# Normalized rows through DRAM and transposed on VectorE in the middle groups, with all weights in the order 8p + c

## The chip, the cores and the metric

The kernel runs on one core of a Trainium2 chip. A core has five engines that run their own instruction queues in order and wait on one another by semaphores: TensorE (PE; its weight loads are listed apart as PEld), VectorE (DVE), ScalarE (ACT), GpSimd (POOL) and SyncE (SP), which here issues nearly all DMA transfers. The metric is the time of one launch on the device in microseconds, as the median of several runs.

## The reference

The input has 16 batches of 128 rows by 1024 columns, and a context of the same shape. The computation is one cross-attention block and one FFN block, both with a residual:

```python
x = x + xattn(layernorm(x), ctx, Wq, bq, Wk, bk, Wv, bv, Wo, bo)
x = x + scale * (ei(layernorm(x)) @ kernel)
# xattn: Q = q @ Wq + bq (32 heads of 32), K, V = ctx @ Wk + bk, ctx @ Wv + bv (8 heads of 32)
#        y = softmax(Q K^T / sqrt(32)) V;  result y @ Wo + bo
# ei:    the last 205 of the 1024 input columns are multiplied by -4
```

Everything is float32; the FFN kernel holds only zeros and ones. A matmul contracts over the 128 partitions, so a row that is to be multiplied by a weight has first to be transposed: its 1024 columns go to 8 chunks of 128 partitions. Which column lies on which partition of which chunk is free, as long as the weight's rows are laid out in the same order.

## The kernel before

**Groups.** Two batches form a group; there are eight groups, 0 to 7. While PE does the attention of group g in four quarters (`attend`: scores `sc`, maximum `negm`, exponentials, `inv` and the division `p`, transposes `tpp`, product `av`), the gaps are filled with dense work from a queue: the output projection of group g-1 (`o_u`, `o_v`, `o_c`), keys and values of group g+1 (`k`, `v`), the FFN of both batches of group g-1 (`f`), and the queries of group g+1 (`q_u`, `q_v`, `q_c`). Query and output projections of a group are Winograd-like: seven products of half-size blocks in place of eight, with sums of weight blocks (`combine`) that are made once on DVE and kept in DRAM.

**Order.** All of it is one manual schedule. `Stream` holds a queue of generators, each of which issues a piece of PE work and yields its supposed length in us, and a list of events (`stream.later(us, fn)`), which issue work of other engines when the supposed clock passes them. So the order of each engine's queue is fixed when the program is built; on the chip each engine takes its instructions in that order and waits where data are not there. `length` is the supposed length of a quarter.

**Rows and their transposes.** A row block of x is loaded (`load_x`), normalized on DVE and POOL in place (`norm_x`, two `bn_stats`, then `normalize`), and transposed on PE: eight 128x128 transposes per batch, four into one PSUM tile `tp_x`, which ACT copies to `xT` (`turned`, line 310). The FFN's rows `x2n` are transposed in the same way (`ffn_transpose`, line 646); ACT copies the PSUM tile `tp_f` to `x2h` and DVE subtracts to get the rest `x2l` (line 649), so that the FFN is two fast matmuls. PSUM tiles `tp_x`, `tp_f`, `tpp` and `av` share one pool of two buffers.

The context is transposed otherwise: it is loaded in four DMAs, each of which brings one quarter of the columns for all 128 rows to one quadrant of 32 partitions (`load_ctx`), so that DVE's transposes of 32x32 blocks (line 319) finish the job. Its tile is ordered [partition, 4 row blocks, 8 chunks, 32 columns], so each 32x32 block is contiguous in a partition. The rows of Wv and Wk are brought to the matching order in four DMAs each (`load_by_quadrants`); Wq and the FFN kernel have the order c*128 + p.

**The queue of transfers.** SP issues in order. Weight pieces of 512 KB (`piece`, a ring of eight) are fetched as earlier ones are used up (`fetch`), in the query and output projections. Each SP transfer signals one of eight semaphores in turn and waits for the transfer that used that semaphore before, eight places ahead of it.

In a middle group the dense work is added in this order:

```python
once(get_x, nxt * GB, 14.0),
once(prep_ctx, nxt, 3.7, 8.0, 13.0, 18.0),
os[grp - 1],
once(get_ctx, nxt + 1),
prep_k(nxt),
mixed(prep_v(nxt), chain(ffn_transpose(p0), ffn_transpose(p1)), 1, 2),
once(get_x, nxt * GB + 1, 5.0),
```

and then `ffn(p0)`, `ffn(p1)` with the first half of `prep_x` mixed in, the residual loads, the second half of `prep_x` and the queries `qs[nxt]`. So the first x row is loaded before the output projection and normalized 14 us of supposed time later; the second after the values.

Of the kernel before, what the change touches and what calls it, by code (L numbers as in the profile page):

```python
# [17 lines left out]
P = 128  # L18
# [64 lines left out]
def kernel(  # L83
# [67 lines left out]
    def load_ctx(b, queues=(nc.sync,)):  # L151
        c_t = work.tile([P, NB, NC, 32], FP, tag="ctx", name=f"ctx{b}", bufs=2)
        src = key_value[b].rearrange("(t r) (k c f) -> k r t (c f)", r=32, k=NB, c=NC)
        for k in range(NB):
            dst = c_t[k * 32 : (k + 1) * 32].rearrange("r t c f -> r t (c f)")
            queues[k % len(queues)].dma_start(out=dst, in_=src[k])
        cs[b] = c_t

    def load_by_quadrants(dst, w, queues):
        src = w.rearrange("(k c f) n -> k f c n", k=NB, f=32)  # L160
        for k in range(NB):
            queues[k % len(queues)].dma_start(out=dst[k * 32 : (k + 1) * 32], in_=src[k])

    def load_x(b):

        x_t = work.tile([P, D], FP, tag="xn", name=f"xn{b}", bufs=3)
        nc.sync.dma_start(out=x_t, in_=x[b])
        xns[b] = x_t
# [16 lines left out]
    load_by_quadrants(wv_sb, Wv, two)  # L185
    load_ctx(1, two)
    load_by_quadrants(wk_sb, Wk, two)
# [33 lines left out]
    def q_block(r, o, k):  # L221

        src = Wq.rearrange("(r c p) n -> r p c n", r=2, p=P)[r]
# [20 lines left out]
    def load_ffn():  # L244
        fw = ffn_w.rearrange("(c p) n -> p c n", p=P)
# [5 lines left out]
    def convert_ffn():  # L251

        row_w = const.tile([P, 1], FP, name="row_w")
        nc.gpsimd.memset(row_w, 1.0)
        nc.gpsimd.affine_select(
            out=row_w,
            in_=row_w,
            compare_op=ALU.is_ge,
            fill=w_inh,
            base=n_exc % P - 1,  # L260
            pattern=[[0, 1]],
            channel_multiplier=-1,
        )
        def chunk_(c):
            raw = raws[c // (NC // 2)][:, c % (NC // 2)]
            if (c + 1) * P <= n_exc:
                nc.scalar.copy(wf_sb[:, c], raw)
            else:
                w = w_inh if c * P >= n_exc else row_w
                nc.scalar.activation(wf_sb[:, c], raw, AF.Copy, scale=w)  # L270

        for c in range(NC):
            stream.later(2.0 * c, lambda c=c: chunk_(c))

# [25 lines left out]
    def turned(store, srcs, grp, h, name, batches=range(GB)):  # L300
# [3 lines left out]
        for j in batches:  # L304
# [3 lines left out]
            for c in range(HC):  # L308
                at = (h * HC + c) * P
                nc.tensor.transpose(tp[:, c], src[:, at : at + P], ident)  # L310
# [3 lines left out]
    def turn_ctx(b, h):  # L314
        grp, j = b // GB, b % GB
        if (grp, h) not in cTs:
            cTs[grp, h] = work.tile([P, HC, T], FP, tag="tT", name=f"cT{grp}_{h}", bufs=3)
        src = cs.pop(b) if h == 1 else cs[b]
        nc.vector.transpose(
            cTs[grp, h][:, :, j * S : (j + 1) * S].rearrange("p c (t n) -> p t c n", t=NB),  # L320
            src[:, :, h * HC : (h + 1) * HC],
        )
# [9 lines left out]
    def chunk(store, grp, c):  # L332
        return store[grp, c // HC][:, c % HC]

# [216 lines left out]
    def weighted(b, a, pts):  # L551
# [11 lines left out]
        yTs[b, a] = work.tile(S4, FP, tag="yT", name=f"yT{b}_{a}", bufs=7)  # L563
# [4 lines left out]
    def out_proj(grp):  # L568
# [12 lines left out]
        def run():  # L581
# [36 lines left out]
            def read(mm, c):  # L618
# [7 lines left out]
                if c in ("c12", "c21"):  # L626
                    x2n = work.tile([P, D], FP, tag="xn", name=f"x2n{b0 + j}", bufs=3)
                    x2ns[b0 + j] = x2n
                    us = 3.0 if c == "c12" else 4.5
                    stream.later(us, lambda: normalize(x2n, x_t, stats[j], f"f{b0 + j}"))  # L630
# [4 lines left out]

    def ffn_transpose(b):

        hi = work.tile([P, NC, S], FR, tag="x2h", name=f"x2h{b}", bufs=2)
        lo = work.tile([P, NC, S], FR, tag="x2l", name=f"x2l{b}", bufs=2)
        src = x2ns.pop(b)  # L640
        x2Ts[b] = (lo, hi)
        for h in range(NC // 4):
            tp = ps_tp.tile([P, 4, P], FP, tag="tp", name=f"tp_f{b}_{h}")
            for j in range(4):
                c = 4 * h + j
                nc.tensor.transpose(tp[:, j], src[:, c * P : (c + 1) * P], ident)  # L646
            cut = slice(4 * h, 4 * h + 4)
# [284 lines left out]
```

## Time and profile before

| What | Value |
|---|---|
| time, median of 3 runs | 819.83 us (819.57 to 819.86) |
| the profiled execution: its time, its span | 817.83 us, 816.1 us |
| granted TensorE clock | 1.000 |
| PE busy with matmuls | 789.8 us (97%) |
| PE transposes `tp_x`, line 310 | 128, 18.2 us busy |
| PE transposes `tp_f`, line 646 | 128, 19.3 us busy |
| DVE transposes of the context, line 319 | 32 of 128x512, 698 ns each |
| ACT copies `xT` and `x2h` | 32 each of 128x512, 590 ns each |
| DVE subtraction `x2l`, line 649 | 32 of 128x512, 692 ns each |
| x rows, issue to landing | 16 of 512 KB, median 5.4 us |
| context quadrants, issue to landing | 128 KB, median 5.9 us |
| stores of out, issue to landing | 512 KB, median 2.7 us |

The page lists busy time by engine, the span in 40 slices, the DMA queues, the chain of work that ended last, the costliest groups of instructions, and the transfers. Beside it the trace gives timelines (start, length, engine, line, operation, and in brackets the idle time before it with what ended it), tables of busy time in chosen stretches, and lists of waits. Matmuls are pipelined and the column of their lengths overlaps: what one costs is read from start to start.

### The profile page before, as it was taken

The numbers are of one execution on the slowest core, as the hardware profiler recorded it, in microseconds if no ns is written. First come the engines' busy times: TensorE is split into PE (matmuls) and PEld (weight loads), VectorE is DVE, ScalarE is ACT, GpSimd is POOL, SyncE is SP. The second block draws the span as 40 slices with busy tenths as digits, with TensorE's granted clock in tenths as the row PEclk, the third lists the DMA queues.
The fourth block names the chain that finished last, engine by engine and source line by source line (L and its number), as shares of the span: only waits on it lengthen the run. The fifth ranks groups of instructions, "written<-read, shape, count | busy, mean of one in ns | idle before, by whom it ended". The sixth has DMA issues, their size and how long they took to land.

```text
span 816.1 us, 13885 instructions
## 1 busy us (share of the span) xinstructions
PE 789.8 (97%) x5216; PEld 593.4 (73%) x5216; DVE 459.9 (56%) x862; ACT 332.7 (41%) x1281; POOL 69.6 (9%) x109
## 2 busy tenths in 40 slices
PE   3997999999999999999999999999999999999998
PEld 3886884678947797488965889568894779756556
DVE  1369748554475554755456454765348565467442
ACT  0243854444334443345333544344434454366200
POOL 1000003002000020000300002000200002000300
PEclk9999999999999999999999999999999999999999
DMA  9999598715885178741887328780578307761511
GB/s 202 357 319 317 198 399 326 210 52 182 273 269 164 43 238 274 262 130 44 286 269 253 80 103 280 276 242 29 179 262 281 132 27 274 246 215 69 195 62 77
DMA packets 81075, 165.14 MB, mean 202 GB/s; under 512 B 5969, under 2 KB 42833, under 8 KB 81009
## 3 DMA queue, kind: packets, MB, share of 16 engines
q1 hardware_dynamic: 79200, 162.55, 59.6%
q10 hardware_dynamic: 1664, 1.57, 1.1%
q8 instruction: 41, 0.67, 0.3%
q0 software_dynamic: 144, 0.14, 0.1%
q14 instruction: 26, 0.20, 0.1%
HBM read 147.46 MB, written 16.78 MB: 201 GB/s over the span
## 4 chain that ended last, share of the span: by engine, by line
PE 86%; DMA 6%; DVE 3%; issue 2%; SPq 1%; ACT 1%; POOL 0%; ACTq 0%; DVEq 0%; POOLq 0%
PE o_u L607 14%; PE f L293 14%; PE q_u L396 12%; PE o_v L607 7%; PE tpp L546 6%; PE q_v L396 6%; PE k L293 5%; PE v L293 5%; PE sc L513 4%; PE av L556 4%; PE o_c L607 3%; PE q_c L396 3%; DMA wo<-in_L_xattn_Wo_dram 2%; PE tp_f L646 2%; PE tp_x L310 1%
## 5 line engine op out<-in xcount | busy, mean ns | idle before, releaser
L529 ACT ACTIVATE p<-sc,negm 128x128 f32<-128x128 f32 x512 | 181.1, 369 | 155.9 <-DVE negm L525 82.3
L548 ACT COPY pt<-tpp 128x512 f32<-128x512 f32 x128 | 74.8, 590 | 117.1 <-PE tpp L546 116.6
L525 DVE TENSOR_REDUCE negm<-sc 128x4 f32<-128x512 f32 x128 | 87.3, 683 | 39.8 <-PE sc L513 39.8
L293 PE MATMUL f<-wf_sb,x2l 128*128 128x512 f32 x256 | 106.0, 414 | 0.0
L529 ACT ACTIVATION_READ_ACCUMULATOR p<-sc,negm 128x1 f32 x512 | 105.8, 207 | 0.0
L293 PE MATMUL f<-wf_sb,x2h 128*128 128x512 f32 x256 | 101.2, 396 | 0.0
L541 DVE TENSOR_TENSOR p<-p,inv 128x512 f32<-128x512 f32 x128 | 88.6, 692 | 4.4
L546 PE MATMUL tpp<-ident,p 128*128 128x128 f32 x512 | 76.7, 273 | 6.3 <-DVE p L541 4.0
L546 PEld LDWEIGHTS tpp<-ident,p 128*128 128x128 f32 x512 | 61.7, 141 | 28.1 <-issue 20.0
L396 PE MATMUL q_u<-t,piece 128*128 128x128 f32 x672 | 81.2, 276 | 0.0
L396 PEld LDWEIGHTS q_u<-t,piece 128*128 128x128 f32 x672 | 78.0, 192 | 0.2 <-DMA piece<-q 0.2
L293 PE MATMUL v<-wv_sb,cT 128*128 128x256 f32 x256 | 62.6, 387 | 12.3 <-DMA wv_sb<-in_L_xattn_Wv_dram 12.3
L178 POOL TENSOR_TENSOR x<-x,bo_b 128x256 f32<-128x256 f32 x64 | 48.8, 795 | 180.2 <-DMA x<-in_x_dram 160.1
L293 PEld LDWEIGHTS v<-wv_sb,cT 128*128 128x128 f32 x256 | 47.5, 195 | 17.7 <-issue 12.3
L607 PE MATMUL o_u<-piece,yT 128*128 128x512 f32 x128 | 59.1, 603 | 0.0
L607 PE MATMUL o_u<-piece,s 128*128 128x512 f32 x128 | 59.0, 594 | 0.0
L607 PE MATMUL o_v<-piece,s 128*128 128x512 f32 x128 | 59.0, 594 | 0.0
L293 PE MATMUL k<-cT,wk_sb 128*128 128x256 f32 x256 | 57.0, 380 | 0.0
L293 PEld LDWEIGHTS f<-wf_sb,x2l 128*128 128x128 f32 x256 | 48.1, 188 | 11.4 <-issue 1.1
L293 PEld LDWEIGHTS f<-wf_sb,x2h 128*128 128x128 f32 x256 | 48.3, 189 | 10.0 <-issue 0.5
L293 PEld LDWEIGHTS k<-cT,wk_sb 128*128 128x128 f32 x256 | 48.5, 190 | 9.0 <-issue 2.6
L564 ACT COPY yT<-av 128x512 f32<-128x512 f32 x32 | 18.7, 585 | 88.0 <-PE av L556 88.0
(77 smaller groups left out, 949.8 us busy)
## 6 DMA issues: line engine op xcount, KB each, us to landing
piece<-o SPq DMA_DIRECT2D x64, 512.0 KB, 4.4
piece<-q SPq DMA_DIRECT2D x56, 512.0 KB, 4.4
piece<-in_L_xattn_Wq_dram SPq DMA_DIRECT2D x50, 512.0 KB, 4.8
piece<-in_L_xattn_Wo_dram SPq DMA_DIRECT2D x48, 512.0 KB, 4.5
xn<-in_x_dram SPq DMA_DIRECT2D x16, 512.0 KB, 5.4
x<-in_x_dram SPq DMA_DIRECT2D x16, 512.0 KB, 4.9
ctx<-in_ctx_dram SPq DMA_DIRECT2D x60, 128.0 KB, 5.9
out_dram<-x SPq DMA_DIRECT2D x15, 512.0 KB, 2.7
```

What stands on the lines that cost most here:

```text
L178: lambda cut=cut: nc.gpsimd.tensor_add(x_t[:, cut], x_t[:, cut], bo_b[:, cut]) and None,
L293: nc.tensor.matmul(mm, lhsT=lhsT, rhs=rhs, start=k == 0, stop=k == n - 1)
L396: nc.tensor.matmul(mm if part is None else mm[:, part], lhsT=lhsT, rhs=rhs, start=start and n == k == 0, stop=k == len(some) - 1, skip_gro ...
L513: nc.tensor.matmul(tiles[i][:, g], lhsT=qT[rows, g], rhs=kT[rows, a, cols], start=True, stop=True,)
L525: nc.vector.tensor_reduce(negm, tile_, AX.X, ALU.max, negate=True)
L529: nc.scalar.activation(p[:, g], tile_[:, g], AF.Exp, bias=negm[:, g : g + 1], accum_out=total[:, g : g + 1],)
L541: nc.vector.tensor_mul(p, p, inv.unsqueeze(2).to_broadcast([P, NG, S]))
L546: nc.tensor.transpose(tp[:, g], p[:, g], ident)
L548: nc.scalar.copy(pt, tp)
L556: nc.tensor.matmul(mm[i * HD : (i + 1) * HD], lhsT=vs[b][:, h * HD : (h + 1) * HD], rhs=pts[i], start=True, stop=True,)
L564: nc.scalar.copy(yTs[b, a], mm)
L607: nc.tensor.matmul(mm, lhsT=lhsT[:, 2 * k + c], rhs=w[:, c], start=start and k == c == 0, stop=k == c == 1, skip_group_check=True,)
```

## The change

For groups 1 to 5 of the loop, the query rows of the next group (groups 2 to 6) and the FFN rows of batches 0 to 9 are no longer transposed on PE. The normalized row is stored to a DRAM tile, loaded again in four quadrant DMAs like the context, and transposed by DVE, for the queries straight into `xT`, for the FFN into the PSUM tile `tp_f`. The other rows keep their PE transposes. All weights get the row order 8p + c (partition p, chunk c), so Wv and Wk are one DMA each; the transposes now read every eighth column: PE's with `src[:, c::NC]`, DVE's with a step of eight within a partition. Rows and returned rows have two buffers each (`row`, `turn`) where `xn` had three; yT has six in place of seven. The FFN scale tiles are per chunk, and all conversions go through `activation`. The second set of sums of Wo starts 8 us later and is spread wider, quarter lengths change, and the order of the dense work in the middle groups is new.

```diff
     def load_ctx(b, queues=(nc.sync,)):
-        c_t = work.tile([P, NB, NC, 32], FP, tag="ctx", name=f"ctx{b}", bufs=2)
-        src = key_value[b].rearrange("(t r) (k c f) -> k r t (c f)", r=32, k=NB, c=NC)
+        c_t = work.tile([P, NB, 32, NC], FP, tag="ctx", name=f"ctx{b}", bufs=2)
+        src = key_value[b].rearrange("(t r) (k n) -> k r t n", r=32, k=NB)
...
-    def load_by_quadrants(dst, w, queues):
-        src = w.rearrange("(k c f) n -> k f c n", k=NB, f=32)
-        for k in range(NB):
-            queues[k % len(queues)].dma_start(out=dst[k * 32 : (k + 1) * 32], in_=src[k])
-
-    def load_x(b):
-
-        x_t = work.tile([P, D], FP, tag="xn", name=f"xn{b}", bufs=3)
+    def load_x(b, tag="row"):
+
+        x_t = work.tile([P, D], FP, tag=tag, name=f"xn{b}", bufs=2)
...
-    load_by_quadrants(wv_sb, Wv, two)
+    nc.sync.dma_start(out=wv_sb, in_=Wv.rearrange("(p c) n -> p c n", p=P))
     load_ctx(1, two)
-    load_by_quadrants(wk_sb, Wk, two)
+    nc.sync.dma_start(out=wk_sb, in_=Wk.rearrange("(p c) n -> p c n", p=P))
...
-        src = Wq.rearrange("(r c p) n -> r p c n", r=2, p=P)[r]
+        src = Wq.rearrange("(p r c) n -> r p c n", r=2, p=P)[r]
...
-        fw = ffn_w.rearrange("(c p) n -> p c n", p=P)
+        fw = ffn_w.rearrange("(p c) n -> p c n", p=P)
...
+    def through_dram(row, name, then):
+        there = dram.tile([P, D], FP, name=f"dram_{name}")
+        nc.sync.dma_start(out=there, in_=row)
+
+        def back():
+            c_t = work.tile([P, NB, 32, NC], FP, tag="turn", name=f"turn_{name}", bufs=2)
+            src = there.rearrange("(t r) (k n) -> k r t n", r=32, k=NB)
+            for k in range(NB):
+                dst = c_t[k * 32 : (k + 1) * 32].rearrange("r t f c -> r t (f c)")
+                nc.sync.dma_start(out=dst, in_=src[k])
+            stream.later(8.0, lambda: then(c_t))
+
+        stream.later(5.0, back)
+
+    def blocks_turned(dst, c_t, h):
+
+        nc.vector.transpose(
+            dst.rearrange("p c (t n) -> p t c n", t=NB),
+            c_t[:, :, :, h * HC : (h + 1) * HC].rearrange("p t f c -> p t c f"),
+        )
...
-                at = (h * HC + c) * P
-                nc.tensor.transpose(tp[:, c], src[:, at : at + P], ident)
+                nc.tensor.transpose(tp[:, c], src[:, h * HC + c :: NC], ident)
...
+    def turn_x(b):
+
+        grp, j = b // GB, b % GB
+        norm_x(b)
+
+        def turn(c_t, h=0):
+            if (grp, h) not in xTs:
+                xTs[grp, h] = work.tile([P, HC, T], FP, tag="tT", name=f"xT{grp}_{h}", bufs=3)
+            blocks_turned(xTs[grp, h][:, :, j * S : (j + 1) * S], c_t, h)
+            if h == 0:
+                stream.later(1.5, lambda: turn(c_t, 1))
+
+        through_dram(xns.pop(b), f"x{b}", turn)
...
-        yTs[b, a] = work.tile(S4, FP, tag="yT", name=f"yT{b}_{a}", bufs=7)
+        yTs[b, a] = work.tile(S4, FP, tag="yT", name=f"yT{b}_{a}", bufs=6)
...
-                    us = 3.0 if c == "c12" else 4.5
-                    stream.later(us, lambda: normalize(x2n, x_t, stats[j], f"f{b0 + j}"))
+                    us = 2.0 if c == "c12" else 4.0
+
+                    def norm():
+                        normalize(x2n, x_t, stats[j], f"f{b0 + j}")
+                        if b0 + j < B - 3 * GB:
+                            through_dram(x2n, f"f{b0 + j}", lambda c_t: ffn_split(b0 + j, c_t))
+
+                    stream.later(us, norm)
...
+    def split(b, h, tp):
+        lo, hi = (part[:, HC * h : HC * h + HC] for part in x2Ts[b])
+        nc.scalar.copy(hi, tp)
+        nc.vector.tensor_tensor(lo, tp, hi, ALU.subtract)
...
+    def ffn_split(b, c_t, h=0):
+
+        if h == 0:
+            new_parts(b)
+        tp = ps_tp.tile([P, HC, P], FP, tag="tp", name=f"tp_f{b}_{h}")
+        blocks_turned(tp, c_t, h)
+        split(b, h, tp)
+        if h == 0:
+            stream.later(1.7, lambda: ffn_split(b, c_t, 1))
...
-                    spread(combine("o", 1, o_parts[1]), 2.5)
+                    stream.later(8.0, lambda: spread(combine("o", 1, o_parts[1]), 3.0))
...
-            length = 17.4 if first else 24.0 if grp < NGRP - 2 else 22.0
+            length = 23.0 if grp < NGRP - 2 else 22.0
...
-            elif more:
+            elif nxt < NGRP - 1:
                 stream.add(
-                    once(get_x, nxt * GB, 14.0),
                     once(prep_ctx, nxt, 3.7, 8.0, 13.0, 18.0),
                     os[grp - 1],
                     once(get_ctx, nxt + 1),
+                    once(get_x, nxt * GB, 5.0, turn_x),
+                    prep_k(nxt),
+                    once(get_x, nxt * GB + 1, 5.0, turn_x),
+                    prep_v(nxt),
+                    ffn(p0),
+                    ffn(p1),
+                    once(residuals, grp),
+                    qs[nxt],
+                )
...
+                if first:
+
+                    length = (17.4, 22.4, 16.0, 14.0)[q]
                 pts = attend(b, a, length)
```

Group 6 keeps PE transposes, with its second x row loaded right after the output projection.

## The prediction, written before the result was known

> **What bounds the kernel now.** The page's first part comes first, then its slices, then one period cut out by a table of stretches, then engine timelines inside that period. In every reading below T is the end of an output projection; in the period shown T = 348.2 us.
>
> ```profile
> PE 789.8 (97%) x5216; PEld 593.4 (73%) x5216; DVE 459.9 (56%) x862; ACT 332.7 (41%) x1281; POOL 69.6 (9%) x109
> ...
> DMA  9999598715885178741887328780578307761511
> ```
>
> TensorE (PE) is busy nearly throughout; the last row repeats a pattern about every five slices, full in the projections and almost empty between. One period of the middle, and a piece of its start-up:
>
> ```profile
> 320.10:417.60 97.50, 97.50 (x665) 74.14 (x665) 55.20 (x104) 40.53 (x158) 8.32 (x12) 1.00 0.60 195
> 352.00:355.00 3.00, 3.00 (x16) 2.64 (x15) 2.20 (x7) 2.59 (x15) 0.55 (x1) 1.00 1.07 231
> 362.00:363.00 1.00, 1.00 (x8) 0.87 (x8) 0.36 (x1) 0.00 (x0) 0.00 (x0) 1.00 0.91 352
> 0.00:10.00 10.00, 0.00 (x0) 0.00 (x0) 1.30 (x2) 0.00 (x0) 3.03 (x11) 1.00 0.88 167
> ```
>
> Columns: stretch, length, busy time of PE, weight loads, DVE, ACT, POOL, then granted clock, DMA share, GB/s. PE has no gap in a 97.5 us period, at full clock, so a middle group lasts as long as its PE work. Quadrant loads of the context (32 partitions, 1 KB packets) move 231 GB/s, a whole x row 352.
>
> PE's timeline gives the price of a transpose, DVE's that of a normalization, and the SP queue's where transfers are issued:
>
> ```profile
> 381.78 0.60 PE L310 MATMUL tp_x<-ident,xn 128*128 128x128 f32 x4
> 382.22 0.60 PE L546 MATMUL tpp<-ident,p 128*128 128x128 f32 x4
> ...
> 353.65 0.81 DVE L285 TENSOR_SCALAR x2n<-x,mv_f,rs_f 128x1024 f32<-128x1024 f32 x1 [0.73 <-POOL rs_f L284]
> ...
> 368.87 1.27 DVE L276 BATCH_NORM_STATS2 st_a<-xn 128x6 f32<-128x512 f32 x2
> 370.18 0.21 DVE L280 BATCH_NORM_AGGREGATE mv_a<-st_a 128x2 f32<-128x12 f32 x1
> ...
> 371.31 0.81 DVE L285 TENSOR_SCALAR xn<-xn,mv_a,rs_a 128x1024 f32<-128x1024 f32 x1 [0.73 <-POOL rs_a L284]
> ...
> 348.80 5.16 SPq L156 DMA_DIRECT2D ctx<-in_ctx_dram  x8
> 360.94 0.35 SPq L167 DMA_DIRECT2D xn<-in_x_dram  x1
> ```
>
> Four transposes hold PE for 0.44 us, from one start to the next; the 0.60 in the column of durations overlaps its successor. A norm is 3.25 us from first statistic to end. The second FFN row is ready at 354.5 = T+6.3. The eight context loads are issued from T+0.6, the second x row only at T+12.7, in an empty queue.
>
> **The change, part by part.** *PE transposes removed.* In groups 1 to 5, 16 transposes of 128x128 for queries and 16 for the FFN: 8 sets of four at 0.44 = 3.5 us per group, 17.6 us in all, if nothing else ends later. A rule weighs in here: the Trainium skill, "VectorE: DVE Perf Modes", section "The three transpose paths", gives 390 ns for one TensorE transpose of 128x128 and 311 ns on VectorE (both bf16), so VectorE should be the place and 32 transposes would save 12.5 us per group. The row says 110 ns each, because they are pipelined; VectorE's set of four takes 698 ns in the groups by line. The row decides: 3.5 us, not 12.5.
>
> *DVE work added.* Per group 8 transposes of 128x512. They, and the 4 of the context, now read with a step of 8 floats, which no row shows. Near row: 698 ns contiguous. The skill's "SBUF — State Buffer", section "Door 1: The DMA port swizzle", states 16-byte lines and a penalty for each access that enters a new one; at a 32-byte step every element does. That rule speaks against the change. Its size is not given; I estimate a doubled slope: adds of 128x256 and 128x512 take 423 and 690 ns, so 512 elements cost 534 ns over a fixed part, and 698 becomes 1230. A full hit by the rule adds 12x0.53 = 6.4 us of DVE per group, none adds 0. I take 1.0 us. DVE's sum, 55.2 + 8x1.0 + 4x0.3 = 64 of 97.5 us, bounds nothing; its order does.
>
> *The new chain.* Before, x rows were loaded well ahead of their use. In the changed program's order, after T: SP issues the store of FFN row 0, eight context loads, x row 0, the store of FFN row 1, four loads back, then the store of x row 0 (waits for its norm), and only behind that x row 1. DVE has: norm of FFN row 1, norm of x row 0, the fourth `inv`/`p` of the running softmax, one `v`, norm of x row 1, and only then the first FFN transpose. So PE waits for softmax and FFN behind two x loads in series.
>
> - x row 0. An SP transfer waits for the one eight places ahead. The first context load (issued T+0.6, 6.4 us to landing in the trace) stands behind 512 KB of store, about 1.4 us at 352 GB/s: landed T+8.4. Then the x load: 3.5 us alone, as the second x row had it, and about 0.6 behind the remaining context: T+12.5. DVE has been idle since T+6.3. Norm: T+15.8; `inv`, `p` 0.9: T+16.7.
> - PE wants that `p` after k (6.9), three sets (1.3), one v and a quarter of the other (4.3): about T+12.6. Stall 4.1.
> - x row 1 is issued at T+16.2, lands 4.0 later (3.5 and half a microsecond behind the store): T+20.2; norm T+23.5; FFN transpose 1.0, ACT copy 0.7, DVE subtraction 0.8: T+26. PE would be ready at T+17.7 (one more set 0.4, rest of v 2.6, `av` 1.0, `sc` 1.1) plus the 4.1: stall 4.2.
> - Second half of that row: `v` 0.4, transpose 1.0, copy 0.7, subtraction 0.7: T+28.8. PE's first eight matmuls end at T+27.9. Stall 0.9.
> - Next late: the read of `f` (748 ns) that frees the PSUM buffer for the second row's FFN. Ahead of it on DVE are two FFN transposes with their splits, a maximum and two x transposes, the first of them on a load that could not start before its buffer was freed at T+27.4 (two tiles carry tag "turn"): landed T+31.7. The read ends at T+36.9, PE is there at T+34.4. Stall 2.5.
>
> Sum 11.7 us against 3.5 saved: +8.2 per group, five groups, **+41 us**. Each later group starts its own chain at its own T, so no group repays another. The bounds, by the same steps: x row 0 landed at T+6.3, when DVE is free, with transposes at 0.70 leaves 0 + 1.8 + 0.6 + 1.5 = 3.9, +0.4 per group or +2; landed at T+14 with transposes at 1.23 gives 5.6 + 4.4 + 1.2 + 3.4 = 14.6, +55.
>
> *Start.* Wv and Wk come as whole 128-partition transfers. The first 10 us move 167 GB/s and PE starts v at 12.3 us. 1 MB at 231 to 352 GB/s takes 4.5 or 3.0 us, twice: 1.5 to 3 us sooner for k; before the slow first stretch (167) up to 3 more. I take -4 (0 to -8).
>
> *Rest.* The other 96 PE transposes load their weights with a step of 8; no row shows it (141 ns contiguous). From 0 to as much again as their 110 ns: 0 to +10.6; I take +2.5. Delaying the second set of Wo sums takes DVE work out of 70 to 90 us, where PE waited 3.4 us for a `p`: -2 (0 to -4). Quarter lengths, smaller yT pool, the FFN scale on ACT (ACT is 41% busy) and the residual packets: 0, hidden behind PE, which has no gap there.
>
> Sum: +41 - 4 + 2.5 - 2 = +37.5. The profiled execution took 817.83 us (span 816.1 and 1.7 around it), 2 below the median of 819.83; the difference is put on the median: **857 us**.
>
> **Rivals.** *Short waits* (20%): x row 0 lands at T+9 and the strided transposes keep 0.70 us. The stalls are then 0.6, 3.9, 0.6 and 1.5: 6.6, +3.1 per group, +15.5; with the rest 832. For it: a landing of an x row takes 5.4 us in the median, and the last context load was issued at T+5.5. Against it: the context's 1 MB at 231 GB/s stands before that row.
>
> *Faster* (12%): the chain at its shortest, decided by one thing, the landing of x row 0: at or before T+6.3 the middle costs only +2, and the start decides: -4 to -8 there and -2 to -4 at the Wo sums give 810 to 816. With no wait for x at all the full -17.6 would be reached, about 798. For it: DMA is nearly empty from T+8 on. Against it: the context loads alone are issued until T+5.8 and the x load stands behind them.
>
> *Steps of 32 bytes cost more than a doubling* (8%): at 2.5 us per transpose, the chain has six of them ahead of the `f` read: +9 per group, some 900.
>
> *The change does nothing* (3%, within 0.2%, 1.6 us, about what a measurement tells from no change): the saving and the stalls cancel.
>
> **How the numbers follow.** The forecast's case has 57%. Slower takes it, the short waits and the dear steps: 85%. Faster 12, same 3. The range runs from 814, inside the faster case, to 886 (+55 with the dearer ends of the rest), leaving out the 900s and the lower half of the faster case.
>
> **What would show it.** In the changed profile: a period of 103 to 108 us in groups 1 to 5; DVE idle before x statistics (`st_a`) ended by a DMA of x, twice per group, 3 to 6 us each; PE gaps before the fourth `tpp`, before the first `f` and between FFN rows; `tp_f` and `tp_x` each with 48 PE transposes left. DVE's transposes at 0.70 or 1.23 us decide the step. Wrong if DVE reaches the FFN transposes without waiting for x, or if PE stays gapless at a period of 94 us.

## The result and the profile after

The changed kernel takes 871.55 us (median of 4 runs, 869.37 to 874.01), 1.064 times the time before (95% interval 1.061 to 1.067). Its profiled execution took 870.12 us, with a span of 868.1 us against 816.1: 52.0 us more.

The first part of the page, with the clock and DMA slices of its second part:

```profile
PE 796.7 (92%) x5056; PEld 593.9 (68%) x5056; DVE 517.2 (60%) x902; ACT 322.8 (37%) x1261; POOL 73.6 (8%) x111
...
PEclk9999999999998999998999889998899999999999
DMA  9989697836778367792777827779268714773331
```

PE has lost its 97%, and its granted clock, which was full throughout, dips once in most groups. PE issues 160 matmuls fewer, as intended, but is not less busy: some of its work ran slower.

One middle group, from the start of an output projection (0.07 us behind its first `o_u`) to the next, then two short stretches inside it, then the first 10 us (columns: stretch, length, busy time of PE, weight loads, DVE, ACT, POOL, granted clock, DMA share, GB/s):

```profile
339.70:447.48 107.78, 98.51 (x633) 73.86 (x633) 66.06 (x112) 38.25 (x154) 8.65 (x12) 0.95 0.69 215
384.00:388.00 4.00, 2.49 (x8) 2.24 (x9) 1.67 (x4) 0.59 (x1) 0.00 (x0) 0.61 0.65 214
396.00:400.00 4.00, 4.00 (x10) 3.13 (x10) 2.77 (x3) 1.14 (x2) 0.00 (x0) 0.50 0.41 122
0.00:10.00 10.00, 0.00 (x0) 0.00 (x0) 2.06 (x2) 1.28 (x1) 3.03 (x11) 1.00 0.73 216
```

The output projections of the five groups that the change rewrites, and of the group behind them, start at 125.64, 232.39, 339.63, 447.41, 556.98 and 665.84 us: 108.0 us per group on average (106.8 to 109.6), where it was 97.5 in each (124.94 to 612.61). That is +10.5 per group and +52.5 in all. The first of these projections starts 0.7 us later than before, and from the last start to the end it takes 202.3 us where it took 203.5. So the whole loss is in the middle groups. In the group shown PE idles 107.78 - 98.51 = 9.3 us.

In that group T, the end of the output projection, is 367.82 (the start of `k`, as in the prediction). The timelines of PE, of DVE and of the SP queue (start, length, engine, line, operation; in brackets the idle time before and what ended it):

```profile
367.82 5.34 PE L313 MATMUL k<-cT,wk_sb 128*128 128x256 f32 x24
...
385.51 1.08 PE L576 MATMUL tpp<-ident,p 128*128 128x128 f32 x4 [4.99 <-DVE p L571]
386.39 3.69 PE L313 MATMUL v<-wv_sb,cT 128*128 128x256 f32 x12
...
395.71 0.80 PE L313 MATMUL f<-wf_sb,x2l 128*128 128x512 f32 x1 [3.54 <-DVE x2l L681]
396.30 0.63 PE L313 MATMUL f<-wf_sb,x2h 128*128 128x512 f32 x1
...
406.92 0.50 PE L313 MATMUL f<-wf_sb,x2l 128*128 128x512 f32 x1 [0.74 <-DVE x L713]
```

```profile
376.18 0.81 DVE L305 TENSOR_SCALAR x2n<-x,mv_f,rs_f 128x1024 f32<-128x1024 f32 x1 [2.61 <-DMA dram_f<-x2n]
...
381.29 1.29 DVE L296 BATCH_NORM_STATS2 st_a<-xn 128x6 f32<-128x512 f32 x2 [4.30 <-DMA xn<-in_x_dram]
...
384.67 0.69 DVE L571 TENSOR_TENSOR p<-p,inv 128x512 f32<-128x512 f32 x1
...
390.04 1.29 DVE L296 BATCH_NORM_STATS2 st_a<-xn 128x6 f32<-128x512 f32 x2 [4.34 <-DMA xn<-in_x_dram]
...
393.22 1.10 DVE L290 STREAM_TRANSPOSE tp_f<-turn_f 128x512 f32<-128x512 f32 x1
394.97 0.69 DVE L681 TENSOR_TENSOR x2l<-tp_f,x2h 128x512 fp32r<-128x512 f32 x1 [0.65 <-ACT x2h L680]
...
406.16 0.71 DVE L713 SCALAR_TENSOR_TENSOR x<-f,fscale,x 128x512 f32<-128x512 f32 x1
```

```profile
368.86 7.55 SPq L156 DMA_DIRECT2D ctx<-in_ctx_dram  x8
376.63 0.35 SPq L162 DMA_DIRECT2D xn<-in_x_dram  x1
...
384.58 0.34 SPq L276 DMA_DIRECT2D dram_x<-xn  x1
385.01 0.38 SPq L162 DMA_DIRECT2D xn<-in_x_dram  x1
385.44 2.24 SPq L283 DMA_DIRECT2D turn_f<-dram_f  x4
```

The chain reads off in order. The eight context loads hold the SP queue to 376.4; the first x row is issued at 376.63 and its statistics start at 381.29 (T+13.5). PE gets the `p` that DVE computes behind that norm 4.99 us late. The second x row is issued only at 385.01, behind the store of the first; its statistics start at 390.04 (T+22.2), and PE waits 3.54 us for the first `x2l`. The second row's FFN then waits for DVE's read of an `f` tile (406.16) and starts at 406.92 (T+39.1). After the two long waits PE works slowly: four `tpp` transposes take 1.08 in place of 0.60 us, twelve `v` matmuls 3.69 in place of 2.76, and `f` matmuls start 0.43 us apart where they had been 0.23 apart; the granted clock is 0.61 and 0.50 in these stretches. That slowness was in no step of the prediction.

### The profile page after: what moved, and what is told of

It reads as the page before. It is cut to its first block, busy times and chain, and to the rows that moved or that the text cites. A ratio compares the mean times of both kernels' runs of the same rounds, so it can differ in the third digit from the quotient of the medians.

```text
span 868.1 us, 13734 instructions
## 1 busy us (share of the span) xinstructions
PE 796.7 (92%) x5056; PEld 593.9 (68%) x5056; DVE 517.2 (60%) x902; ACT 322.8 (37%) x1261; POOL 73.6 (8%) x111
## 4 chain that ended last, share of the span: by engine, by line
PE 68%; DMA 13%; DVE 11%; ACT 3%; issue 3%; SPq 1%; POOL 1%; DVEq 0%; POOLq 0%; ACTq 0%
PE q_u L426 11%; PE o_u L637 11%; PE f L313 9%; PE o_v L637 6%; DMA xn<-in_x_dram 6%; PE q_v L426 6%; PE tpp L576 5%; DMA ctx<-in_ctx_dram 4%; PE sc L543 3%; PE av L586 3%; PE o_c L637 3%; PE q_c L426 3%; PE q L313 3%; DVE tp_f L290 2%; DMA turn_x<-dram_x 2%
## 5 line engine op out<-in xcount | busy, mean ns | idle before, releaser
L313 PE MATMUL f<-wf_sb,x2l 128*128 128x512 f32 x256 | 111.1, 434 | 24.2 <-DVE x2l L681 17.3
L313 PE MATMUL f<-wf_sb,x2h 128*128 128x512 f32 x256 | 106.2, 415 | 0.0
L576 PE MATMUL tpp<-ident,p 128*128 128x128 f32 x512 | 79.4, 280 | 27.6 <-DVE p L571 24.4
L571 DVE TENSOR_TENSOR p<-p,inv 128x512 f32<-128x512 f32 x128 | 91.0, 711 | 4.4
L313 PE MATMUL v<-wv_sb,cT 128*128 128x256 f32 x256 | 70.4, 430 | 13.2 <-DMA wv_sb<-in_L_xattn_Wv_dram 11.6
L313 PEld LDWEIGHTS f<-wf_sb,x2l 128*128 128x128 f32 x256 | 51.8, 202 | 39.9 <-DVE x2l L681 19.6
L173 POOL TENSOR_TENSOR x<-x,bo_b 128x256 f32<-128x256 f32 x64 | 52.3, 847 | 251.8 <-DMA x<-in_x_dram 250.5
L313 PEld LDWEIGHTS v<-wv_sb,cT 128*128 128x128 f32 x256 | 54.8, 223 | 22.4 <-issue 11.5
L313 PEld LDWEIGHTS f<-wf_sb,x2h 128*128 128x128 f32 x256 | 51.7, 202 | 10.6 <-issue 0.5
L680 ACT CAST x2h<-tp_f 128x512 fp32r<-128x512 f32 x32 | 18.7, 590 | 100.0 <-DVE tp_f L290 59.9
```

The costliest lines, as they stand in the source:

```text
L173: lambda cut=cut: nc.gpsimd.tensor_add(x_t[:, cut], x_t[:, cut], bo_b[:, cut]) and None,
L313: nc.tensor.matmul(mm, lhsT=lhsT, rhs=rhs, start=k == 0, stop=k == n - 1)
L571: nc.vector.tensor_mul(p, p, inv.unsqueeze(2).to_broadcast([P, NG, S]))
L576: nc.tensor.transpose(tp[:, g], p[:, g], ident)
L680: nc.scalar.copy(hi, tp)
```

## The experiments

### The late x rows alone, without the DRAM trip

The kernel before, with the loads of the x rows put where the change has them; all transposes stay on PE.

```diff
-                    once(get_x, nxt * GB, 14.0),
                     once(prep_ctx, nxt, 3.7, 8.0, 13.0, 18.0),
                     os[grp - 1],
                     once(get_ctx, nxt + 1),
+                    once(get_x, nxt * GB, 5.0),
                     prep_k(nxt),
+                    once(get_x, nxt * GB + 1, 5.0),
                     mixed(prep_v(nxt), chain(ffn_transpose(p0), ffn_transpose(p1)), 1, 2),
-                    once(get_x, nxt * GB + 1, 5.0),
```

> The kernel before with one part of the change alone: in the middle groups the two x rows are loaded where the change loads them, behind the context loads after the output projection, and behind the keys; all transposes stay on PE and nothing goes through DRAM. My theory: the wait for x alone costs most of what the change cost: VectorE waits 3 to 5 us for the first row, PE waits for the fourth softmax tile and its clock falls; the period rises from 97.5 to 101 to 106 us, time 840 to 865 us. Rival (the harm comes with the way through DRAM): the period stays within 1 us of 97.5, time 815 to 825 us.

Measured: 844.6 us (one run), a period of 101.9 us, clock 0.993. One group of it, in the same columns as above:

```profile
327.94:429.75 101.81, 98.42 (x668) 73.94 (x665) 55.45 (x104) 40.81 (x158) 8.26 (x12) 1.00 0.59 186
```

No row went through DRAM here, and the place of the loads alone costs 4.4 us per group, 22 us in the five groups. (The whole time is some 25 us higher, since the edit reaches the sixth group too, which takes 97.3 us in place of 92.5.) So the place of the loads explains less than half of the +10.5 us per group; the theory had said most. The rest appears only with the trip: in the changed kernel the second x load stands behind the store of the first, and the FFN transposes stand behind its norm on DVE. That reading comes from the timelines above; the next run bears on it from the other side.

### The x rows one group ahead

In the changed kernel each pair of x rows is loaded, normalized and stored during the queries of the group before; only the loads back stay where the change has its x work.

```diff
-                    once(get_x, nxt * GB, 5.0, turn_x),
+                    once(later_x, 10.0, nxt * GB),
                     prep_k(nxt),
-                    once(get_x, nxt * GB + 1, 5.0, turn_x),
+                    once(later_x, 10.0, nxt * GB + 1),
                     prep_v(nxt),
                     ffn(p0),
                     ffn(p1),
                     once(residuals, grp),
+                    once(ahead, nxt + 1),
                     qs[nxt],
...
+        def later_x(us, b):
+            stream.later(us, lambda: bring_x(b))
+
+        def ahead(grp):
+            if grp < NGRP - 1:
+                for j in range(GB):
+                    get_x(grp * GB + j, 8.0 + 8.0 * j, turn_x)
```

(`turn_x` ends with the store; `bring_x` is its second half, the loads back and the transposes.)

> The changed kernel with one thing moved: the two x rows of a middle group are loaded, normalized and stored in the query stage of the group before; the loads back, the transposes on VectorE and the FFN's way through DRAM stay. My theory (two x loads in series stand in VectorE's order ahead of the softmax and of the FFN): the period of the middle groups falls from 108 us to 94 to 97, no wait of VectorE for an x load is left there, the granted clock returns to about 1.00, and the time is 803 to 818 us. Rival A (VectorE is too slow with 12 strided transposes per group): the period stays above 104, time over 850 us. Rival B (the way through DRAM itself, store and load back, is late): the waits of VectorE move from x to the returned FFN rows and the period stays above 101, over 835 us.

Measured: 825.82 us (825.04 to 828.62), 1.0094 of before (1.0062 to 1.0127); the period is 97.5 us, clock 0.993. With the x loads and their norms off the chain 10.5 us per group are gone, though the trip and all strided DVE transposes stay, so the chain through them is the cause of the middle's loss. The parts do not add up singly: late rows alone cost 4.4 us per group, the trip without late rows nothing once its 3.5 us of saved PE work are counted, both together 10.5 with that saving counted. The expected 94 to 97 was just missed, and so was the time of 803 to 818. Two things are left over. One pair of rows now falls into the first group, where DVE stands in front of them and PE with it:

```profile
106.34 1.09 PE L591 MATMUL tpp<-ident,p 128*128 128x128 f32 x4 [8.71 <-DVE p L586]
```

That puts the first projection at 133.25 instead of 125.64 us. And in each of the four periods with moved norms PE still waits 2.8 to 4.1 us, mostly in pieces of 0.3 to 1.4: for `x2l`, for the `f` read, and in the queries for `qT` reads that now stand behind those norms. In the fifth period, which loads no x row ahead, the waits are 0.7 us and the period is 95.05.

### Contiguous DVE transposes

The DVE transposes of the changed kernel read 32 neighbouring elements instead of every eighth. The columns then come out in another order than the weights' rows, so the result is another one; the amount of work is the same.

```diff
+        flat = c_t.rearrange("p t f c -> p t (f c)").rearrange("p t (c f) -> p t c f", c=NC)
         nc.vector.transpose(
             dst.rearrange("p c (t n) -> p t c n", t=NB),
-            c_t[:, :, :, h * HC : (h + 1) * HC].rearrange("p t f c -> p t c f"),
+            flat[:, :, h * HC : (h + 1) * HC],
         )
```

> The changed kernel with VectorE's transposes reading contiguous blocks of 32 in place of every eighth float; the columns then come out in another order than the weights', all else is the same. My theory: a transpose takes 0.70 us instead of 1.10 to 1.16, which shortens the chain only behind the second x load, by about four transposes ahead of the last wait: 1 to 2 us per period, time 861 to 867 us. Rival (VectorE's speed is the cause): the period falls by 6 us or more, under 842 us.

Measured: 858.14 us (one run), 13.4 below the changed kernel. DVE's transposes by group of instructions, the changed kernel first (operation, count, busy time, mean ns of one), then this one:

```profile
L290 DVE STREAM_TRANSPOSE cT<-ctx 128x512 f32<-128x512 f32 x32 | 34.7, 1095 | 11.7 <-DMA ctx<-in_ctx_dram 11.7
L290 DVE STREAM_TRANSPOSE tp_f<-turn_f 128x512 f32<-128x512 f32 x20 | 22.8, 1142 | 0.0
L290 DVE STREAM_TRANSPOSE xT<-turn_x 128x512 f32<-128x512 f32 x20 | 22.8, 1160 | 0.7 <-DMA turn_x<-dram_x 0.4
```

```profile
L291 DVE STREAM_TRANSPOSE cT<-ctx 128x512 f32<-128x512 f32 x32 | 22.0, 698 | 12.0 <-DMA ctx<-in_ctx_dram 12.0
L291 DVE STREAM_TRANSPOSE tp_f<-turn_f 128x512 f32<-128x512 f32 x20 | 14.2, 708 | 0.0
L291 DVE STREAM_TRANSPOSE xT<-turn_x 128x512 f32<-128x512 f32 x20 | 13.5, 695 | 3.0 <-DMA turn_x<-dram_x 3.0
```

A step of 32 bytes costs 0.40 to 0.47 us per transpose. The period fell from 108.0 to 106.4, as expected, 8 us in the five groups. Another 3.7 us lies ahead of the first projection (121.92), which the expected 861 to 867 had not counted; 0.8 of it is an earlier first `v` and 1.1 a wait of the second group's k for the transposed context, which is gone; the rest is not traced. The step is a side cost: the waits for x stay.

### The clock's share: PE kept busy through its waits

In the group above PE's clock fell after waits of 3.5 and 5 us. These two kernels put idle fp32 matmuls into the PSUM buffers just before the fourth `tpp` and the first `f`, which overwrite them: first ten and eight of 0.86 us, then five and four (as below). The trace records each of them as two.

```diff
         tp = ps_tp.tile([P, NG, S], FP, tag="tp", name=f"tpp_{b}_{a}_{i}")
+        if i == 3 and a == 0 and b % GB == 1 and GB < b < B - 2 * GB:
+            warm(tp.rearrange("p g n -> p (g n)"), 5)
...
             mm = ps_mm.tile([P, HALF], FP, tag="mm", name=f"f_{b}_{h}")
+            if h == 0 and b % GB == 0 and b < B - 3 * GB:
+                warm(mm, 4)
```

> The changed kernel with matmuls that nobody reads, in groups 1 to 5: ten ahead of the transposes of the fourth softmax tile of the second quarter, eight ahead of the first FFN product; they write the tile that is overwritten next. PE waits as long as before but is not idle. Theory that part of the loss is PE's clock, which falls after the long waits: the granted clock returns to 0.99 or 1.00, the work after the waits takes its usual time (0.23 us per FFN matmul instead of 0.43), and the period falls by 3.5 to 5 us, time 847 to 855 us. Rival (the clock falls for another reason, or the chain on VectorE decides and a faster PE only waits again): the period falls by less than 2 us, time over 862 us.

Measured: 874.27 us (one run), clock 0.997, where the rival puts it (over 862). But the idle work (8.6 and 6.9 us) was longer than the waits it filled, so this run says nothing of the clock's share.

> The changed kernel with idle matmuls into an unused result put in front of the fourth set of tpp (five of 0.86 us, where PE idles 4.99 us) and of the first f (four of 0.86 us, where it idles 3.54): all of them fit into the idle time, nothing else is changed. If the lower clock after the waits is a cost of its own, about 4.5 us per group, the period falls from 108 to 103.5 to 105 us and the time to 850 to 857. If the clock is only a sign of the waits and costs nothing beside them, the period stays at 107 to 109 and the time at 868 to 874.

Measured: 869.63 us (one run), clock 0.991, a mean period of 108.1 us. PE's timeline of one group (T is 368.58 here; the filler matmuls are the lines of L575):

```profile
381.12 4.45 PE L575 MATMUL tpp<-wk_sb,ident 128*128 128x512 f32 x10
386.13 0.66 PE L584 MATMUL tpp<-ident,p 128*128 128x128 f32 x4 [0.56 <-DVE p L571]
386.62 2.76 PE L313 MATMUL v<-wv_sb,cT 128*128 128x256 f32 x12
...
391.40 3.70 PE L575 MATMUL f<-wk_sb,ident 128*128 128x512 f32 x8
396.03 0.50 PE L313 MATMUL f<-wf_sb,x2l 128*128 128x512 f32 x1 [0.92 <-DVE x2l L689]
...
398.80 0.51 PE L313 MATMUL f<-wf_sb,x2l 128*128 128x512 f32 x1 [0.66 <-DVE x2l L689]
...
407.22 0.50 PE L313 MATMUL f<-wf_sb,x2l 128*128 128x512 f32 x1 [2.63 <-DVE x L723]
...
408.27 0.63 PE L313 MATMUL f<-wf_sb,x2l 128*128 128x512 f32 x1
408.70 0.63 PE L313 MATMUL f<-wf_sb,x2h 128*128 128x512 f32 x1
```

The fillers did what they should: twelve `v` take 2.76 us again, and the clock is 1.00 from 384 to 388 and from 396 to 400. But the mean period did not move. What PE gained it waited off at the next step: the two later waits are 0.66 and 2.63 us, where the changed kernel had none and 0.74. From the second row's statistics to the start of its FFN it takes 16.8 to 16.9 us in four of the five groups here (18.4 in the other), and 16.8 to 16.9 in all five groups of the changed kernel, with the clock low after its waits. DVE's chain decides when, however fast PE works in between.

The same mean is partly chance. The second x row landed 0.9 us sooner here on average, and in two groups, the one shown among them, the clock fell behind the last wait, where no later wait takes the loss up: `f` matmuls again start 0.43 us apart, and from the second row's FFN to the next projection it takes 42.1 us in place of 40.5. In the changed kernel that stretch takes 40.5 us in all five groups. So its slow stretches only filled time in which PE would have waited; as a cost of its own the clock is nothing there.

### The context's loads behind

```diff
-                    once(get_ctx, nxt + 1),
                     once(get_x, nxt * GB, 5.0, turn_x),
                     prep_k(nxt),
                     once(get_x, nxt * GB + 1, 5.0, turn_x),
                     prep_v(nxt),
                     ffn(p0),
+                    once(get_ctx, nxt + 1),
```

> The changed kernel with the eight context loads of a middle group issued after the first row's FFN, in place of before the first x row; nothing else is moved. If the serial chain of the two x loads sets the period (first x row lands at T+8 in place of T+13.5, everything behind it moves forward by 4 to 6 us, the third and later waits shrink less), the period falls from 108 to 100 to 103 us and the time to 832 to 847. If the waits came from the clock, the strided transposes or the loads competing for the DMA engines, the chain moves but the period stays above 105 and the time above 856.

Measured: 850.55 us (850.41 to 852.46), 1.038 of before (1.036 to 1.040), a period of 104.7 us: faster than the changed kernel, but between the two forecasts (100 to 103, and above 105). DVE, the SP queue and PE of one group (T is 361.18):

```profile
369.69 1.28 DVE L296 BATCH_NORM_STATS2 st_a<-xn 128x6 f32<-128x512 f32 x2 [0.36 <-DMA xn<-in_x_dram]
...
380.51 1.29 DVE L296 BATCH_NORM_STATS2 st_a<-xn 128x6 f32<-128x512 f32 x2 [6.42 <-DMA xn<-in_x_dram]
```

```profile
369.77 2.22 SPq L283 DMA_DIRECT2D turn_f<-dram_f  x4
372.97 0.34 SPq L276 DMA_DIRECT2D dram_x<-xn  x1
373.36 0.43 SPq L162 DMA_DIRECT2D xn<-in_x_dram  x1
373.83 2.25 SPq L283 DMA_DIRECT2D turn_f<-dram_f  x4
```

```profile
386.19 0.79 PE L313 MATMUL f<-wf_sb,x2l 128*128 128x512 f32 x1 [6.96 <-DVE x2l L681]
...
397.38 0.50 PE L313 MATMUL f<-wf_sb,x2l 128*128 128x512 f32 x1 [1.20 <-DVE x L713]
```

The first x row now comes 5.0 us sooner (T+8.5) and the softmax no longer waits here. The second is issued 5.0 us sooner too (T+12.2), but its statistics start 7.15 us after the issue, where that took 5.03 in the same group of the changed kernel. So they start at T+19.3, 2.9 us sooner, and the period of this group is 104.87, 2.9 us shorter. The five groups, in order, from the timelines of both kernels:

| | changed kernel | context behind |
|---|---|---|
| statistics of the second x row, us after T | 21.3, 21.7, 22.2, 24.0, 23.3 | 19.4, 18.1, 19.3, 19.4, 19.8 |
| from there to the second row's FFN | 16.8 to 16.9 | 16.8 to 17.0 |
| period | 106.75, 107.23, 107.79, 109.57, 108.86 | 104.91, 103.57, 104.87, 105.07, 105.24 |

The landing of the second x row sets the period, one for one. What sets that landing stays open. More transfers stand close around it here, the store and eight quadrant loads of 128 KB. But in the changed kernel the same store and four quadrant loads are issued around it in every group, and from issue to statistics it took 4.5 to 7.3 us.

### The order 8p + c alone

The kernel before with all weights, PE transposes and context transposes in the new order, and nothing stored to DRAM.

```diff
-    load_by_quadrants(wv_sb, Wv, two)
+    nc.sync.dma_start(out=wv_sb, in_=Wv.rearrange("(p c) n -> p c n", p=P))
...
-                at = (h * HC + c) * P
-                nc.tensor.transpose(tp[:, c], src[:, at : at + P], ident)
+                nc.tensor.transpose(tp[:, c], src[:, h * HC + c :: NC], ident)
```

> The kernel before with all weights, PE transposes and context transposes in the order 8p + c, and nothing through DRAM. My prediction: the start gives 4 us back and strided weight loads cost 2.5 us, so 816 to 820. Reading of the changed trace: the start gave nothing and the strided loads cost nothing, so 818 to 822 with a period of 97.5. Rival: the strided steps are dear, PE's weight loads of 190 ns show in the set of four and the context's transposes of 1.1 us delay k and v, so over 825.

Measured: 816.46 us (815.87 to 817.5), 0.9958 of before (0.9943 to 0.9972): 3.3 us faster. PE's first `v` starts at 11.27 us instead of 12.29, and the period is 97.41 instead of 97.53. PE's transposes by group of instructions, of the kernel before and then of this one:

```profile
L310 PEld LDWEIGHTS tp_x<-ident,xn 128*128 128x128 f32 x128 | 14.4, 140 | 6.3 <-ACT xT L311 3.3 <-ACT pt L548 0.9
```

```profile
L311 PEld LDWEIGHTS tp_x<-ident,xn 128*128 128x128 f32 x128 | 18.0, 195 | 5.4 <-ACT xT L312 3.1 <-ACT pt L549 1.1
```

Weight loads with a step of eight take 195 ns in place of 140, and the period shows no cost: they overlap the matmuls. The two profiled executions differ by only 0.4 us in span, so where the 3.3 us lie is only partly seen. The start varies: the first `v` began at 12.27 and 12.29 us in the two profiles with quadrant loads of the weights, and between 8.91 and 11.77 in the nine with whole loads.

### Finding the place for the x rows

Two versions of the x-ahead kernel try to lose its leftovers. The first moves the norms into the FFN (shown), and also transposes the returned rows 1.5 us sooner and takes the first pair out of the first group:

```diff
-                    once(get_ctx, nxt + 1),
                     once(later_x, 10.0, nxt * GB),
                     prep_k(nxt),
                     once(later_x, 10.0, nxt * GB + 1),
+                    once(get_ctx, nxt + 1),
                     prep_v(nxt),
                     ffn(p0),
+                    once(ahead, nxt + 1),
                     ffn(p1),
                     once(residuals, grp),
-                    once(ahead, nxt + 1),
                     qs[nxt],
```

> x rows normalized and stored one group ahead as in the run that loaded x ahead, with four further shifts: those norms during the FFN in place of the queries, the context's loads behind the returned rows, the returned rows transposed 1.5 us sooner, and the first pair of x rows inside the second group's output projection in place of the first group. If the remaining PE waits (4.1 us per group, 7.6 us in the first group) came from the order of the transfers and of DVE alone, the period falls from 98 to 94 to 96 us and the first period starts at 126 us, so 800 to 812. If DVE's added work (8 x 1.14 us) can't be hidden wherever it is put, the period stays at 97 or above and the time is 815 or more.

Measured: 840.17 us (838.49 to 841.28), 1.025 of before (1.023 to 1.027); the first projection starts at 124.11, even before the expected 126, but the period is 102.4, not 94 to 96. POOL's timeline, and a DVE and a PE line beside it:

```profile
408.54 0.73 POOL L173 TENSOR_TENSOR x<-x,bo_b 128x256 f32<-128x256 f32 x1 [7.59 <-DMA x<-in_x_dram]
409.91 0.73 POOL L173 TENSOR_TENSOR x<-x,bo_b 128x256 f32<-128x256 f32 x1 [0.65 <-DMA x<-in_x_dram]
410.60 0.55 POOL L313 TENSOR_TENSOR rs_a<-ve_a,minus_half 128x1 f32<-128x1 f32 x1
```

```profile
411.18 1.20 DVE L314 TENSOR_SCALAR xn<-xn,mv_a,rs_a 128x1024 f32<-128x1024 f32 x1 [5.84 <-POOL rs_a L313]
```

```profile
414.77 5.47 PE L441 MATMUL q_v<-t,piece 128*128 128x128 f32 x32 [3.49 <-DVE qT L543]
```

POOL computes each norm's `rs_a` in order, and now additions to the residual rows stood ahead of it, which waited for their loads. So the second norm held DVE for 5.84 us, and DVE held the query products. The low clock costs real time here: PE has no further wait behind those 32 `q_v` in this group, and they take 5.47 us where the same 32 took 3.84 in the x-ahead kernel.

The second version puts the norms where DVE has room and nothing of POOL stands ahead: inside the output projection of the group itself.

```diff
+                    once(ahead, nxt),
                     once(prep_ctx, nxt, 3.7, 8.0, 13.0, 18.0),
                     os[grp - 1],
-                    once(get_ctx, nxt + 1),
                     once(later_x, 10.0, nxt * GB),
                     prep_k(nxt),
                     once(later_x, 10.0, nxt * GB + 1),
                     prep_v(nxt),
                     ffn(p0),
+                    once(get_ctx, nxt + 1),
                     ffn(p1),
                     once(residuals, grp),
-                    once(ahead, nxt + 1),
                     qs[nxt],
...
-                    get_x(grp * GB + j, 8.0 + 8.0 * j, turn_x)
+                    get_x(grp * GB + j, 12.0 + 6.0 * j, turn_x)
...
-            stream.later(8.0, lambda: then(c_t))
+            stream.later(6.5, lambda: then(c_t))
```

> x rows loaded and normalized inside the output projection of the group that uses them last (loaded at its start, stored before the FFN rows are), returned during k and v; the context's loads behind all returned rows; returned FFN rows transposed 1.5 us sooner. If nothing but the order of DMA and DVE kept the 3.5 us per group from showing, the period is 94 to 95.5 us and the time 798 to 808. If DVE's 8 x 1.14 us of added transposes still make a read of f or q late, the period is 96 to 98 and the time 810 to 820.

Measured: 799.17 us (798.2 to 801.73), 0.9755 of before (0.9726 to 0.9784): faster than both kernels, and inside what was expected. One group, and the first part of its page:

```profile
311.86:406.14 94.28, 94.06 (x637) 70.78 (x633) 65.71 (x112) 38.08 (x154) 8.67 (x12) 1.00 0.76 246
```

```profile
PE 774.8 (97%) x5056; PEld 579.9 (73%) x5056; DVE 513.9 (64%) x902; ACT 321.8 (40%) x1261; POOL 73.4 (9%) x111
```

PE has almost no gap again (94.06 of 94.28 us) at full clock, and the mean period is 94.2 us, 3.4 below the 97.5 of before and 3.2 below the 97.4 of the order 8p + c alone: about the predicted 3.5 us of saved transposes. The strided DVE transposes are all in it (66 of 94 us) and cost nothing. DVE's added work was never the bound; its order was.

## Why the prediction was right, and where it missed

The forecast was slower, 857 us within 814 to 886; the time is 871.55. Direction and mechanism hold.

*The saving.* 3.5 us per group was right: the last version shows 3.4. The 12.5 us that the rule set aside would have given did not come.

*The chain.* Right in kind: two x loads in series on the SP queue, behind the context, with softmax and FFN waiting on DVE behind their norms. Taking the loads off the chain takes 10.5 us per group away.

*The term that was mis-sized* is the landing of the two x rows. The forecast had T+12.5 and T+20.2; over the five groups the statistics start at T+13.2 and T+22.5 on average. The first row was issued at T+7.9 (forecast T+8.4) and took 5.3 us (4.1). The early issue hides a reading that was too long: the first context load was put at 6.4 us to landing, and in the five groups before it took 5.4 to 6.1. The second row was issued at T+16.9 (T+16.2) and took 5.6 (4.0), from 4.5 to 7.3. The step counted half a microsecond for the store ahead of it and nothing for the four quadrant loads issued 0.4 us behind it; whether these are the reason is not shown. The last step, where the second row's FFN starts, came at T+39.4 on average in place of T+36.9. That lateness accounts, within 0.2 us, for the 2.3 us between +10.5 and the forecast's +8.2, and 5 x 2.3 = 11.5 us.

*The split into stalls* was wrong in a way that did not matter for the sum. Forecast were 4.1, 4.2, 0.9 and 2.5 us; the group shown has 4.99, 3.54, none and 0.74. The missing time is PE at half clock after the first two, which the forecast did not foresee. That the sum did not need it was luck, not argument. The Trainium skill, "TensorE: Matmul & The Clock Gate", section "Why this matters for your kernels", warns of exactly that: no idle gaps of PE beyond some 3 us between bursts, or the clock halves. The trace agrees (granted clock 0.61 and 0.50 in the stretches around the ends of gaps of 4.99 and 3.54 us), but the limit is not sharp: in the run with fillers a gap of 2.63 us spaced the next `f` matmuls 0.43 apart in one group, and gaps of 2.63 and 2.65 us left them at 0.23 in two others. Added to the sum, the rule would have put some 4.5 us per group, 22 in all, on top. The runs show that this would have been wrong here: with and without the low clock the second row's FFN starts 16.8 to 16.9 us after its statistics, so the clock's loss fell into time in which PE would have waited for DVE.

*DVE's strided transposes.* Taken 1.0 us, measured 1.10 to 1.16, between no cost (0.70) and the doubled slope (1.23), and nearer to the latter. The run with contiguous reads puts their cost at 1.9 us per group behind the second row's landing (15.0 us to its FFN in place of 16.9); 1.6 of it shows in the period, where that row landed 0.3 us later.

*Start and rest.* Forecast -4 for the start, -2 for the later sums of Wo and +2.5 for strided weight loads of PE, together -3.5; measured +0.7 before the first projection and -1.2 behind the last rewritten group, together -0.5. In this profile `v` began 0.7 us sooner (11.56), and the first 10 us moved 216 GB/s where it was 167; over all profiles with whole weight loads `v` began 0.5 to 3.4 us sooner, so the step had the right sign and was mostly too large. The saving was used up again before the first projection, which starts 114.1 us behind that `v` where it was 112.7; the strided context's 1.1 us wait is part of it. The sums of Wo were not tested alone. The strided weight loads showed no cost. With 11.5 from the chain these 3.0 us close the account: 37.5 + 11.5 + 3.0 = 52.0.

*An unforeseen wait.* DVE held the second FFN row for 2.61 us behind the store of the first. It cost nothing here, since DVE then waited 4.30 us for x anyway.

*The rivals.* The short waits needed the first x row at T+9. The run with the context behind gave just that (T+8.4 to T+9.0), and the period was still 104.7, not 100.6. The rival also had transposes at 0.70 us, which the contiguous run prices at 1.9 of these 4.1; the rest is the second row, which by the forecast's steps would have come at T+16.7 and came at T+19.2 on average. Transposes beyond a doubling and no change are out. For the fast end, "no wait for x at all" was put at about 798; the last version has that and took 799, with 16.8 us saved in the middle (forecast 17.6) and 1.2 us at each end.

## What to carry to other kernels

A wait in series is priced by its last link: follow the chain on the slower engine to the point where the bound engine joins it for the last time, and give each transfer on it a spread: the same load, with the same transfers issued around it, took 4.5 to 7.3 us. Idle gaps and a falling clock on PE are then not added to that; they lie inside it, unless nothing waits behind them. When work moves from the bound engine to one with room, put its inputs where that engine has nothing else waiting behind them, and look at every queue they cross, the small one of POOL too.

## What the hardware showed unexpectedly

DVE's transpose of 128x512 fp32 with a step of 32 bytes took 1.10 to 1.16 us against 0.70 contiguous. PE's weight loads with that step took 195 ns against 140, and the period showed none of it. A 512 KB load of an x row, with one store ahead and four quadrant loads of 128 KB behind, took 4.5 to 7.3 us from issue to use in the five groups of one profile. And where POOL's additions ran beside DVE, a normalization took 1.20 us against 0.81.
